# A four-part transformer kernel on one core: short last key blocks in two matmul passes, and the second batch's layer norm in smaller steps

## The chip, the cores and the metric

The kernel runs on one core of one Trainium2 chip. The metric is the device time of one execution in microseconds (us); of several runs the median is taken. The engines are called as the profile calls them: PE (matmuls; PEld is its loading of weights), DVE, ACT, POOL, and SP, whose queue issues most DMAs here.

## What is computed

The input x has 2 batches of 1024 tokens with 512 features, all in float32. Two layers follow each other; each normalises x and adds an attention and a feed-forward part to it:

```python
xn = layernorm(x)
x = x + attn0(xn) + ffn0(xn)      # one head of 128; streams mixed by a 50-step Sinkhorn chain
xn = layernorm(x)
x = x + attn1(xn) + ffn1(xn)      # 32 heads; experts by a gate
```

The change lies in the second layer's attention and in the normalisation ahead of it:

```python
q = (xn @ Wq.T)                                   # 32 heads of 128
k = (latents_k @ Wk_up.T); v = (latents_v @ Wv_up.T)   # 8 key/value heads, each for 4 query heads
scores = q @ k.T / sqrt(128);  scores = where(causal, scores, -1e9)
out = softmax(scores) @ v
x = x + out @ Wo.T + ffn1(xn)
```

The gate of ffn1 chooses two of eight experts for each token, with a capacity that is counted over both batches, so the gate of the second batch has to be known before ffn1 of the first can be computed.

## The kernel before

**Numbers in two halves.** Matmuls take float16 operands, and a float32 operand is held as a high and a low float16 part. A product needs three passes (`PASSES`, L81): high x high, high x low and low x high.

**The second layer's attention** (`layer1_attn`, L766) goes through 16 groups: 8 key/value heads for each of 2 batches. A group has 32 row steps. Row step s takes 32 queries of each of the group's 4 heads (128 rows) against the W = 32(s + 1) keys that the causal mask leaves:

- PE computes the scores (L88) into PSUM, and DVE takes the row minimum of the negated scores (L283, L287).
- ACT takes the exponential with its row sum (L291). DVE takes the reciprocal (L302).
- `rows_hi` (L301): ACT writes the high part of the normalised row (L308). `rows_lo` (L310): DVE writes the low part (L314), POOL fills what is left of the last block of 128 keys with zeros (L319), and SP transposes both parts by DMA (L320). W keys take m = ceil(W / 128) blocks of 128 for each part, 2m blocks in all.
- `attn_out` (L341) multiplies the transposed rows with the values, with V as weights, in three passes for each block of 128 keys; each matmul has 256 columns, two row steps of 128 rows (L345). `group_av` (L741) calls it for half k = 0 or 1 of query tile c: for k = 0 the two row steps have 32 and 64 keys in their last block, for k = 1 they have 96 and 128.
- ACT and DVE take the result out of PSUM in two halves (L104, L105), and PE multiplies it with Wo (L88); DVE adds it to `acc` (L737).

**What sets the order.** Beside the row steps stands a list of things to do (`fill`): each has a group and a step in which it is put, by hand. So the projections of the next group, the splitting of its weights and all the rest of the second batch's first layer are strewn over the first batch's 8 groups. `put(0, s, f)` (L1044) takes a step s counted from the first group; group 6 begins at step 192, group 7 at 224. A scheduler then orders each engine's instructions from this program. `behind(i, j, True)` (L192) makes instruction i wait for j; `last_low[0]` is the latest L314.

**The second batch's normalisation.** After the last mixing of the streams (`mix0_units`, L596, which loads each tile of x into a buffer of the tag xr, of which there are four), `late_norm` (L1038) takes the statistics of all 8 tiles at step 198 (L219, L220) and their scale and shift. At steps 200 to 207 `tile_of` (L1006) makes the transposed normalised tiles for the gate by way of `normed_T` (L227): POOL normalises (L235), ACT writes the high part into an xr buffer (L238), POOL the low part (L240), and SP transposes (L242). Three steps later each tile's gate product follows (L859). The gate's chain on DVE goes on to step 220, where `weights_of` (L916) counts both batches. At steps 231 to 238 `xT_tile` (L1002) makes the tiles again for good, half of them on POOL and half on DVE, and from 240 the latents of the second batch follow.

**Also met in the prediction:** a bias is added in the first layer's attention by matmuls with a single row (`row`, L484), followed by ordinary ones (L486).

Of the kernel before, what the change touches and what calls it, by code (L numbers as in the profile page):

```python
# [9 lines left out]
F16 = mybir.dt.float16  # L10
# [6 lines left out]
P = 128  # L17
# [19 lines left out]
FP = ((0, 2, 0, 2, 0, 2, 0, 2), (2, 2, 2, 2, 2, 2, 2, 2))  # L37
X1 = 7
CA, CB, CC, CD = 4, 1, 1, 3
SK0, SKN, MX0, MXN, LN1 = 1, 116, 122, 74, 198  # L40

G0, G1, GL, WT, LX, LA = 16, 200, 3, 220, 231, 240
AVD, WOD = 5, 10
KVN, QN, QNN, QH = 19, 18, 24, 1
FW, FF = 210, 221
BS, BP, BV = 4, 3, 1
CQ, CV = (0, 1), (0, 0)
PSCALE = 16384.0
# [3 lines left out]
def tile_model(ctx: ExitStack, tc: tile.TileContext, out: bass.AP, a: dict):  # L52
# [11 lines left out]
    def T(tag, shape, dt=F32, bufs=None):  # L64
        count[0] += 1
        kw = {} if bufs is None else {"bufs": bufs}
        return sb.tile(shape, dt, tag=tag, name=f"{tag}_{count[0]}", **kw)
# [124 lines left out]
    def behind(i, j, wait=False):  # L192

        kind = mybir.DependencyClass.Sync if wait else mybir.DependencyClass.NoSync
        tc.add_manual_dep(i.ins, j.ins.name, mybir.DependencyInfo(
            kind, mybir.DependencyReason.DATA), reason="behind")
# [14 lines left out]
        rs = C(f"rs{tag}{b}", [P, 3, NT])  # L211
        return mv, rs

    def layernorm_tiles(b, mv, rs, ts):
        ve = T("ve", [P, NT], bufs=2)
        sl = slice(ts[0], ts[-1] + 1)
        for t in ts:
            st = T("bnst", [P, 6], bufs=2)
            V.bn_stats(st, acc[b, t])  # L219
            V.bn_aggr(mv[:, t, :], st)  # L220
        V.tensor_scalar(ve[:, sl], mv[:, sl, 1], LN_EPS, None, ALU.add)
        rsqrt(rs[:, 0, sl], ve[:, sl], "rs")
        V.tensor_scalar(rs[:, 2, sl], rs[:, 0, sl], 4.0, None, ALU.mult)
        return V.scalar_tensor_tensor(rs[:, 1, sl], mv[:, sl, 0], -1.0, rs[:, 2, sl],
                                      ALU.mult, ALU.mult)

    def normed_T(b, mv, rs, t, dst, pool, tags=(("f2k", FB), ("wo", WB))):  # L227

        xn = T(tags[0][0], [P, NC, P], bufs=tags[0][1])
        xf = xn.rearrange("p c d -> p (c d)")  # L230
        hl = T(tags[1][0], [P, NC, 2, P], F16, bufs=tags[1][1])
        if pool > 1:
            A.activation(xf, acc[b, t], AF.Identity, scale=rs[:, 2, t:t + 1], bias=rs[:, 1, t:t + 1])
        elif pool:
            G.tensor_scalar(xf, acc[b, t], rs[:, 2, t:t + 1], rs[:, 1, t:t + 1], ALU.mult, ALU.add)  # L235
        else:
            V.tensor_scalar(xf, acc[b, t], rs[:, 2, t:t + 1], rs[:, 1, t:t + 1], ALU.mult, ALU.add)
        last_hi[0] = A.activation(hl[:, :, 0, :], xn, AF.Copy)  # L238
        eng = G if pool in (1, 2) else V
        lo = eng.tensor_tensor(hl[:, :, 1, :], xn, hl[:, :, 0, :], ALU.subtract)  # L240
        (last_pool if eng is G else last_lo)[0] = lo
        last_T[0] = nc.sync.dma_start_transpose(dst, hl.rearrange("p c l d -> p (c l d)"))  # L242

    def proj_T(w, xT, half):

# [20 lines left out]
    def share(got, n, k, make):  # L266

        if k % n == 0:
            got[0] = make()
        return got[0][:, k % n]  # L270
# [23 lines left out]

    def rows_parts(W, n, k):

        m = -(-W // P)
        hl = share(hl_of, n, k, lambda: T("Phl", [P, n, 2 * S // n], F16, bufs=LB))
        return hl[:, :2 * m * P].rearrange("p (l k) -> p l k", l=2)

    def rows_hi(Pm, r, W, pool, hl):  # L301
        V.reciprocal(r[:, 1:2], r[:, 0:1])  # L302
        A.activation(r[:, 1:2], r[:, 1:2], AF.Copy, scale=PSCALE)  # L303
        if pool:
            A.activation(Pm[:, :W], Pm[:, :W], AF.Copy, scale=r[:, 1:2])
            A.activation(hl[:, 0, :W], Pm[:, :W], AF.Copy)
        else:
            A.activation(hl[:, 0, :W], Pm[:, :W], AF.Copy, scale=r[:, 1:2])  # L308

    def rows_lo(Pm, r, W, pool, hl, dst):  # L310
        if pool:
            G.tensor_tensor(hl[:, 1, :W], Pm[:, :W], hl[:, 0, :W], ALU.subtract)
        else:
            lo = V.scalar_tensor_tensor(hl[:, 1, :W], Pm[:, :W], r[:, 1:2], hl[:, 0, :W],  # L314
                                        ALU.mult, ALU.subtract)
            last_low[0] = lo
        if W < hl.shape[2]:

            behind(G.memset(hl[:, :, W:], 0.0), lo)  # L319
        nc.sync.dma_start_transpose(dst, hl.rearrange("p l k -> p (l k)"))  # L320

    pending = []

# [14 lines left out]
        count[0] += 1  # L338
        return ps.tile([P, 512], F32, tag="av", name=f"av_{count[0]}", bufs=BV)

    def attn_out(p, Vh, PT, nj):  # L341

        for j in range(nj):
            for k, (l, r) in enumerate(PASSES):
                nc.tensor.matmul(p, Vh(j, l), PT(r * nj + j),  # L345
                                 start=(j == 0 and k == 0),
                                 stop=(j == nj - 1 and k == 2))


    SC0 = 1.0 / (math.sqrt(128.0) * 1024.0)  # L350
# [321 lines left out]
    def latents(b):  # L672
        cmp[b] = T("cmp", [P, NC, 2, S], F16, bufs=1)

    def lat_w(mc):
        st = T("f2k", [P, NC, P], bufs=FB)
        nc.gpsimd.dma_start(st, a["Wlat"][mc])
        w1 = T("wo", [P, 2, NC, P], F16, bufs=WB)
        split_pool(st, w1[:, 0], w1[:, 1], 32.0)
        return w1  # L680

    def fetch(src):
        st = T("f2k", [P, 512], bufs=FB)
# [54 lines left out]
        if last:  # L738
            nc.scalar.dma_start(out[(b * NT + t) * P:(b * NT + t + 1) * P, :], acc[b, t])

    def group_av(Vh, PT, c, k, p):  # L741


        attn_out(p.rearrange("p (h b q) -> p b h q", h=4, q=QR)[:, 2 * k:2 * k + 2].rearrange(
                     "p b h q -> p h b q"), lambda j, l: Vh[:, l, j, :],
                 lambda n: PT[:, n].rearrange("p b (h q) -> p h b q", q=QR), c + 1)
        if k == 0:
            return None
        ao = T("ao", [P, 2, 4, P], F16, bufs=2)
        hi, lo = [ao[:, l].rearrange("p h q -> p (h q)") for l in range(2)]  # L750
        evac(p, hi, lo, 1.0 / PSCALE)
        return ao
# [13 lines left out]
    def layer1_attn(kv0, start, extra):  # L766
# [8 lines left out]

        kvs, Qs, PTs, avs, aos, wos = [{} for _ in range(6)]

        def q_unit(g, u):
            half, hh = divmod(u, 4)
            if hh == 0:  # L780
                Qs[g, half] = T("Q", [P, 2, NS // 2, 4, QR], F16, bufs=2)
            qproj(g // NG, qw[g, hh], Qs[g, half], hh, half)
# [8 lines left out]
        def av(g, c, k):  # L791
            if k == 0:
                avs[g, c] = out_tile()
            aos[g, c] = group_av(kvs[g]["V"], PTs[g, 2 * c + k], c, k, avs[g, c])

        def wo(g, c):
            wo_block(g // NG, c, aos[g, c], [wos[g, h] for h in range(4)], g % NG == NG - 1)
# [6 lines left out]
        for g in range(N):  # L804
# [14 lines left out]
                    at(g, s, lambda g=g, hh=hh: split_wo(g + 1, hh))  # L819
            for u in range(4):  # L820
                at(g, QH + (1 if (g + 1) % NG == 0 else 3) * u, lambda g=g, u=u: q_unit(g, 4 + u))
            for c in range(NT):
                for k in range(2):
                    at(g, 4 * c + 2 * k + AVD, lambda g=g, c=c, k=k: av(g, c, k))
                at(g, 4 * c + WOD, lambda g=g, c=c: wo(g, c))
# [173 lines left out]
    def new_xT(b):  # L999
        xT1[b] = T("xT", [P, NT, 2 * NC, P], F16, bufs=1)  # L1000

    def xT_tile(b, t, pool):  # L1002
        normed_T(b, *ln1[b], t, xT1[b][:, t], pool, (("f2k", FB), ("wo", WB)) if b else
                 (("xr", XB), ("wo", WB)))

    def tile_of(b, t):  # L1006
        d = T("wo", [P, 2 * NC, P], F16, bufs=WB)
        normed_T(b, *ln1[b], t, d, True, (("f2k", FB), ("xr", XB)))
        return d

    new_xT(0)
# [23 lines left out]
    gw1 = gating_w()  # L1035
    chain = sinkhorn(1, logit[1])

    def late_norm():  # L1038
        ln1[1] = layernorm(1, "b")
        layernorm_tiles(1, *ln1[1], range(NT))  # L1040

    extra = {}

# [11 lines left out]
    for t in range(NT):  # L1055
        for k, f in enumerate(mix0_units(1, t, f0[1][5], True)):
            put(0, MX0 + MXN * (4 * t + max(k - 1, 0)) // 32, f)
    for t in range(NT):
        put(1, 2 * t, lambda t=t: branch0_add(1, t, y4s[t], f0[1][4]))
    hs, gates, dts, lw = {}, {}, {}, {}  # L1060
# [5 lines left out]
    def gate_step(b):  # L1066
        next(gates[b], None)

    for b, s in ((0, G0), (1, G1)):
        put(0, s, lambda b=b: gate_start(b))  # L1070
        for t in range(NT):
            if b == 0:
                put(0, s + t, lambda t=t: gating_h(hs[0], t, gw1, xT1[0][:, t]))
            else:
                put(0, s + t, lambda t=t: dts.update({t: tile_of(1, t)}))
                put(0, s + t + GL, lambda t=t: gating_h(hs[1], t, gw1, dts[t]))
        for k in range(10):
            put(0, s + NT + GL + k, lambda b=b: gate_step(b))
    put(0, LN1, late_norm)
    put(0, WT, weights_of)  # L1080
    put(0, LX, lambda: new_xT(1))
    for t in range(NT):
        put(0, LX + t, lambda t=t: xT_tile(1, t, t % 2 == 1))

    def lat_unit(mc, th):
        if mc + th == 0:
# [1 line left out]
        lat_evac(1, mc, th, lat_block(1, lw[mc], th))  # L1088

    for mc in range(4):  # L1090
        put(0, LA + 2 * mc - 4, lambda mc=mc: lw.update({mc: lat_w(mc)}))
        for th in range(2):
            put(0, LA + 2 * mc + th, lambda mc=mc, th=th: lat_unit(mc, th))
    for k in range(6):
        for s in (FW, 8 * 58 + 2):
            put(0, s + 2 * k - 2, lambda k=k: ffn_fetch(k))
            put(0, s + 2 * k, lambda k=k: ffn_split(k))
    for t in range(NT):
        put(0, FF + t, lambda t=t: ffn_block(0, t))
        put(60, 4 * t + 3, lambda t=t: ffn_block(1, t))  # L1100
# [48 lines left out]
```

## Time and profile before

| | |
|---|---|
| median of 3 runs | 1860.09 us (1855.35 to 1863.01) |
| the profiled execution, its own time | 1855.46 us |
| its span in the profile | 1853.7 us |
| mean granted clock | 0.976 |
| DVE, ACT, POOL busy | 78%, 64%, 49% of the span |
| L345, matmuls with the values | 3648, 447.7 us busy, 274 ns mean |
| L314, low parts of rows | 515, 434.4 us busy, 853 ns mean |
| L319, fills with zeros | 384, 72.6 us busy |
| L320, transposes of rows | 528, 3.2 us median to landing |

A busy time is the sum of the instructions' spans on an engine. Matmuls overlap each other in it, so that 274 ns is how long one of L345 was in the engine, not how far it is from the next. The first layer ends near 250 us, the first batch's eight groups fill the time to about 950 us, and the second batch's the rest.

### The profile page before, as it was taken

What the parts mean: (1) busy time and instruction counts of PE and PEld (TensorE: products, weight loads), DVE (VectorE), ACT (ScalarE), POOL (GpSimd) and SP (SyncE); (2) the same over time, 40 slices, a digit from 0 to 9 for tenths busy, and PEclk for the clock granted to TensorE, in tenths of its full rate; (3) what the DMA queues carried; (4) which work ended last, traced back from release to release, by engine and by line L of the source; (5) the groups of instructions that cost most, each with busy time, mean ns of one, the idle gap of its engine ahead of it and who ended that gap; (6) DMA issues with size and microseconds to landing.
All of it is one profiled execution on the core that took longest, in us unless ns stands there. A gap on an engine that the chain in (4) does not pass through costs nothing. (4 is left out here: it accounts for less than half of the span.)

```text
span 1853.7 us, 35094 instructions
## 1 busy us (share of the span) xinstructions
PE 1715.7 (93%) x11458; PEld 1046.0 (56%) x11458; DVE 1447.6 (78%) x4050; ACT 1194.1 (64%) x2917; POOL 910.6 (49%) x1540
## 2 busy tenths in 40 slices
PE   4756399999999999998999999999999999999998
PEld 3434146566666556655555556666666666656565
DVE  8888978988888877777976867777777777777675
ACT  3848665656676778776544756666666767676554
POOL 5567639768775455647634333424242433335200
PEclk9878699999999999999999999999999999999999
DMA  7435225666574657468546555656565656566455
GB/s 211 82 56 124 67 51 131 143 115 144 113 147 102 143 115 158 111 131 158 137 92 141 130 120 126 146 111 150 107 151 115 142 117 140 117 141 139 101 123 120
DMA packets 707306, 230.26 MB, mean 124 GB/s; under 512 B 689953, under 2 KB 690081, under 8 KB 707122
## 3 DMA queue, kind: packets, MB, share of 16 engines
q1 hardware_dynamic: 691666, 180.75, 47.2%
q0 software_dynamic: 13152, 43.07, 8.5%
q10 hardware_dynamic: 2304, 4.20, 0.7%
q8 instruction: 90, 1.47, 0.4%
q14 instruction: 94, 0.77, 0.1%
HBM read 52.81 MB, written 4.19 MB: 31 GB/s over the span
## 5 line engine op out<-in xcount | busy, mean ns | idle before, releaser
L291 ACT ACTIVATE P<-P,nm 128x1024 f32<-128x1024 f32 (+31 forms) x528 | 391.3, 742 | 250.0 <-DVE nm L283 234.8
L314 DVE SCALAR_TENSOR_TENSOR Phl<-P,r,Phl 128x1024 f16<-128x1024 f32 (+31 forms) x515 | 434.4, 853 | 85.9 <-ACT Phl L308 79.5
L88 PE MATMUL s<-K,Q 128*128 128x512 f16 (+22 forms) x2400 | 440.7, 317 | 19.5 <-DVE P L287 11.6
L345 PE MATMUL av<-PT,V 128*128 128x256 f16 x3648 | 447.7, 274 | 7.5 <-DMA PT<-Phl 6.8
L345 PEld LDWEIGHTS <-V 128*128 128x128 f16 x3648 | 357.0, 98 | 94.7 <-DMA PT<-Phl 8.3
L308 ACT ACTIVATE Phl<-P,r 128x1024 f16<-128x1024 f32 (+31 forms) x515 | 370.0, 731 | 22.3 <-DMA PT<-Phl 3.3
L88 PE MATMUL pp<-xT,wq 128*128 128x512 f16 x1536 | 372.9, 381 | 6.3 <-DVE acc L737 3.2
L88 PE MATMUL pp<-wo,ao 128*128 128x512 f16 x1536 | 369.9, 379 | 2.9 <-ACT ao L104 2.7
L94 POOL TENSOR_SCALAR f2k<-f2k 128x512 f32<-128x512 f32 x164 | 109.5, 668 | 499.9 <-DVE Phl L314 444.5
L88 PEld LDWEIGHTS <-Q 128*128 128x128 f16 x2400 | 223.2, 98 | 178.2 <-issue 28.4
L88 PEld LDWEIGHTS <-wq 128*128 128x128 f16 x1536 | 149.6, 98 | 173.8 <-issue 8.5
L88 PEld LDWEIGHTS <-ao 128*128 128x128 f16 x1536 | 149.4, 98 | 156.5 <-ACT ao L104 4.8
L287 DVE TENSOR_SCALAR_CACHE_REDUCE P<-s 128x512 f32<-128x512 f32 (+15 forms) x272 | 152.6, 562 | 21.7 <-PE s L88 19.7
L283 DVE CUSTOM_DVE_ANT_0 P<-s,mask,nm 128x272 f32<-128x272 f32 (+15 forms) x256 | 157.3, 615 | 8.7 <-PE s L88 1.0
L303 ACT ACTIVATE r<-r 128x1 f32<-128x1 f32 x528 | 96.2, 193 | 66.2 <-DVE r L302 65.4
L319 POOL MEMSET Phl<- 128x192 f16 (+2 forms) x384 | 72.6, 209 | 133.5 <-DMA PT<-Phl 95.7
L302 DVE RECIPROCAL r<-r 128x1 f32<-128x1 f32 x528 | 79.2, 155 | 75.3 <-ACT P L291 72.1
L104 ACT ACTIVATE ao<-av 128x512 f16<-128x512 f32 x128 | 75.1, 587 | 92.2 <-PE av L345 92.0
L283 DVE CUSTOM_DVE_ANT_0 P<-s,mask 128x32 f32<-128x32 f32 (+15 forms) x256 | 104.3, 432 | 27.6 <-PE s L88 27.1
L104 ACT ACTIVATE Q<-pp 128x512 f16<-128x512 f32 x128 | 74.5, 582 | 76.7 <-PE pp L88 72.2
L737 DVE SCALAR_TENSOR_TENSOR acc<-pp,acc 128x512 f32<-128x512 f32 x128 | 87.4, 682 | 41.0 <-PE pp L88 40.6
L105 DVE SCALAR_TENSOR_TENSOR Q<-pp,Q 128x512 f16<-128x512 f32 x128 | 87.6, 684 | 34.9 <-ACT Q L104 34.6
(254 smaller groups left out, 2119.1 us busy)
## 6 DMA issues: line engine op xcount, KB each, us to landing
f2k<-in_Wq POOLq DMA_DIRECT2D x64, 256.0 KB, 3.2
f2k<-in_WoT POOLq DMA_DIRECT2D x64, 256.0 KB, 3.3
PT<-Phl SPq DMA_TRANSPOSE x528, 3.2
acc<-in_x SPq DMA_DIRECT2D x16, 256.0 KB, 4.6
f2k<-in_Wup POOLq DMA_DIRECT2D x16, 256.0 KB, 3.5
out<-acc ACTq DMA_DIRECT2D x16, 256.0 KB, 3.5
xr<-in_x SPq DMA_DIRECT2D x12, 256.0 KB, 4.1
f2k<-in_Wlat POOLq DMA_DIRECT2D x8, 256.0 KB, 5.5
```

The lines of the kernel that those rows point to most:

```text
L88: nc.tensor.matmul(dst, lhs(l), rhs(r), start=(i == 0 and j == 0), stop=(i == n - 1 and j == 2))
L94: first = G.tensor_scalar(stage, stage, scale, 1.0, ALU.mult, ALU.mult)
L104: A.activation(hl_hi, src, AF.Copy, scale=scale)
L105: return V.scalar_tensor_tensor(hl_lo, src, scale, hl_hi, ALU.mult, ALU.subtract)
L283: last_row[0] = V.tensor_tensor_reduce(Pm[:, o:o + w], pt[:, :w], mask[:, 512 - w:], -scale, first, ALU.add, ALU.min, nm[:, k:k + 1])
L287: last_row[0] = V.tensor_scalar(Pm[:, o:o + w], pt[:, :w], -scale, first, ALU.mult, ALU.min, accum_out=nm[:, k:k + 1])
L291: A.activation(Pm[:, :W], Pm[:, :W], AF.Exp, bias=last, scale=-1.0, accum_out=r[:, 0:1])
L303: A.activation(r[:, 1:2], r[:, 1:2], AF.Copy, scale=PSCALE)
L308: A.activation(hl[:, 0, :W], Pm[:, :W], AF.Copy, scale=r[:, 1:2])
L314: lo = V.scalar_tensor_tensor(hl[:, 1, :W], Pm[:, :W], r[:, 1:2], hl[:, 0, :W], ALU.mult, ALU.subtract)
L345: nc.tensor.matmul(p, Vh(j, l), PT(r * nj + j), start=(j == 0 and k == 0), stop=(j == nj - 1 and k == 2))
L737: V.scalar_tensor_tensor(acc[b, t], p, 1.0 / 256.0, acc[b, t], ALU.mult, ALU.add)
```

## The change

**Two passes for a short last block.** Where the last block has at most 64 keys (the first two row steps of every four), `rows_parts` now lays the last block out as 64 columns of high part and 64 columns of low part, so that a row has 2c + 1 blocks instead of 2c + 2 (c full blocks stand before the last). The low part is then written by two DVE instructions where c > 0: one for the full blocks, one for the last. Only rows with 32 keys in the last block have something to fill with zeros. On PE the last block takes two matmuls: one with all 128 rows, whose weights `Vm` hold the high part of the block's first 64 values twice, and one with 64 rows, for the low part of the values. `twice` copies the values for it, by two DMAs on SP for each group, into a buffer of the tag xr.

```diff
     def rows_parts(W, n, k):
+        c, w = divmod(W, P)
+        hl = share(hl_of, n, k, lambda: T("Phl", [P, n, 2 * S // n], F16, bufs=LB))
+        if 0 < w <= 64:
+            hl = hl[:, :(2 * c + 1) * P]
+            o = c * P
+            lo = [(o, W, hl[:, o + 64:o + 64 + w])]
+            if c:
+                lo.insert(0, (0, o, hl[:, o + P:]))
+            pad = hl[:, o:o + P].rearrange("p (l k) -> p l k", l=2)[:, :, w:] if w < 64 else None
+            return hl, hl[:, :W], lo, pad
...
     def rows_lo(Pm, r, W, pool, hl, dst):
...
+        for a0, a1, lo in los:
...
+                last_low[0] = V.scalar_tensor_tensor(lo, Pm[:, a0:a1], r[:, 1:2], hi[:, a0:a1],
+                                                     ALU.mult, ALU.subtract)
+        if pad is not None:
+            behind(G.memset(pad, 0.0), last_low[0])
+        nc.sync.dma_start_transpose(dst[:, :whole.shape[1] // P], whole)
...
+    def attn_out(p, Vh, PT, nj, mixed=None):
+        full = nj - (mixed is not None)
+        todo = [(Vh(j, l), PT(r * nj + j)) for j in range(full) for l, r in PASSES]
+        if mixed is not None:
+            todo += [(mixed, PT(full)), (Vh(full, 1)[:64], PT(full)[:64])]
+        for k, (v, pt) in enumerate(todo):
+            nc.tensor.matmul(p, v, pt, start=(k == 0), stop=(k == len(todo) - 1))
...
+        def twice(g):
+            Vm = kvs[g]["Vm"] = T("xr", [P, NT, P], F16, bufs=XB)
+            for k in range(2):
+                nc.sync.dma_start(Vm[64 * k:64 * k + 64], kvs[g]["V"][0:64, 0])
...
+            at(g, 2, lambda g=g: twice(g))
```

**The second batch's norm.** Each tile's statistics come three steps after its last mixing (`late_stats`); what is left of `late_norm` goes to step 197. Making a tile is cut in two: the normalising and the high part in one step, the low part and the transpose in the next (`later`). POOL's two instructions of a tile wait for the latest L314 (L381 is the new line of L345, L347 that of L314). Tiles 1, 4 and 7 are normalised on ACT instead of POOL, and the steps are no longer one after the other:

```diff
-G0, G1, GL, WT, LX, LA = 16, 200, 3, 220, 231, 240
+G0, GL, WT, LX, LA = 16, 2, 221, 231, 240
+G1 = (198, 199, 200, 201, 203, 204, 205, 207)
+GP = (1, 2, 1, 1, 2, 1, 1, 2)
+G2 = 210
...
-FW, FF = 210, 221
+FW, FF = ((210, 212, 213, 215, 216, 218), tuple(8 * 58 + 2 + 2 * k for k in range(6))), 222
...
-            G.tensor_scalar(xf, acc[b, t], rs[:, 2, t:t + 1], rs[:, 1, t:t + 1], ALU.mult, ALU.add)
+            xg = G.tensor_scalar(xf, acc[b, t], rs[:, 2, t:t + 1], rs[:, 1, t:t + 1], ALU.mult, ALU.add)
+            if later is not None:
+                behind(xg, last_low[0], True)
...
+        def low():
+            lo = eng.tensor_tensor(hl[:, :, 1, :], xn, hl[:, :, 0, :], ALU.subtract)
+            if eng is G and later is not None:
+                behind(lo, last_low[0], True)
+            (last_pool if eng is G else last_lo)[0] = lo
+            last_T[0] = nc.sync.dma_start_transpose(dst, hl.rearrange("p c l d -> p (c l d)"))
...
+        put(0, MX0 + MXN * (4 * t + 3) // 32 + 3, lambda t=t: late_stats(t))
...
-                put(0, s + t, lambda t=t: dts.update({t: tile_of(1, t)}))
-                put(0, s + t + GL, lambda t=t: gating_h(hs[1], t, gw1, dts[t]))
+                put(0, G1[t], lambda t=t: dts.update({t: tile_of(1, t, lambda f: lows.update({t: f}))}))
+                put(0, G1[t] + 1, lambda t=t: lows.pop(t)())
+                put(0, G1[t] + GL + 1, lambda t=t: gating_h(hs[1], t, gw1, dts[t]))
```

The tiles that are made for good (`xT_tile`, step 231 on) are cut in the same way. The weights of the second batch's latents are fetched two steps before they are split, and their splitting waits for the latest L314; the weights of ffn1 are split at slightly other steps for the first batch, and the counting and ffn1 come one step later.

## Prediction

> **What bounds the kernel now.** I read the page's busy shares and slices first, then the busy time by stretch, then TensorE's waits, then the timeline where TensorE changes from one kind of matmul to the next.
>
> ```profile
> PE 1715.7 (93%) x11458; PEld 1046.0 (56%) x11458; DVE 1447.6 (78%) x4050; ACT 1194.1 (64%) x2917; POOL 910.6 (49%) x1540
> ...
> PE   4756399999999999998999999999999999999998
> ```
>
> From slice 7 on PE is full. A busy PE need not be PE at its peak, so I checked by stretches (span; PE, PEld, DVE, ACT, POOL busy; granted clock):
>
> ```profile
> 250.00:820.00 570.00, 558.90 (x3776) 343.67 (x3775) 470.79 (x1318) 402.75 (x1034) 364.79 (x693) 1.00 0.57 124
> 820.00:950.00 130.00, 115.46 (x838) 72.16 (x837) 107.64 (x287) 72.62 (x176) 86.29 (x120) 0.96 0.69 145
> 1090.00:1840.00 750.00, 748.98 (x4995) 464.14 (x4993) 556.45 (x1523) 487.33 (x1168) 252.07 (x466) 1.00 0.60 129
> ```
>
> In the second batch (1090 to 1840) PE idles 1.0 us in 750; in the first (250 to 820) 11.1 us in 570, and DVE is 83% busy there. Between them, where the second batch is normalised, 14.5 of 130 us are idle. The timeline of PE (start, length, group) in a full stretch gives the price of a matmul:
>
> ```profile
> 1458.08 2.78 PE L345 MATMUL av<-PT,V 128*128 128x256 f16 x24
> 1460.70 2.32 PE L88 MATMUL pp<-wo,ao 128*128 128x512 f16 x10
> 1462.86 0.38 PE L88 MATMUL pp<-xT,wq 128*128 128x512 f16 x1
> ```
>
> Start to start, 24 of L345 take 2.62 us: 109 ns each; ten of 512 columns take 2.16 us: 216 ns. That is streaming with nothing between, and whatever shortens PE's stream in these stretches shortens the span.
>
> **Part 1: two passes instead of three.** For each group, query tile and first half (16 x 8 = 128 times) the three 256-column matmuls of the last key block become two. Removed: 128 x 109 ns = **14.0 us**, all on PE.
>
> The second of the two is new in kind: it uses 64 rows, and every matmul around it 128. In the built order each of the 128 stands between 128-row matmuls, so there are 256 changes of row count. No 64-row matmul is in this trace; the nearest rows are the 1-row bias matmuls of L484. PE, then PEld:
>
> ```profile
> 189.42 0.82 PE L345 MATMUL av<-PT,V 128*128 128x256 f16 x6
> 190.17 1.46 PE L484 MATMUL pp<-wo,row 1*128 1x512 f16 x6
> ...
> 192.83 1.03 PE L486 MATMUL pp<-wo,wo 128*128 128x512 f16 x4
> 194.21 0.59 PE L484 MATMUL pp<-wo,row 1*128 1x512 f16 x2 [0.35 <-DVE acc L488]
> 194.73 0.82 PE L486 MATMUL pp<-wo,wo 128*128 128x512 f16 x3
> ```
>
> ```profile
> 193.78 0.09 PEld L484 LDWEIGHTS <-row 1*128 1x128 f16 x1 [0.42 <-issue]
> 194.21 0.09 PEld L484 LDWEIGHTS <-row 1*128 1x128 f16 x1 [0.33 <-issue]
> 194.72 0.33 PEld L486 LDWEIGHTS <-wo 128*128 128x128 f16 x3 [0.42 <-issue]
> ```
>
> Within one row count the next weights load while the matmul before streams: the second L484 load starts at 194.21, with the first matmul. At a change they don't. Into one row: four L486 from 192.83 stream until 192.83 + 4 x 0.216 = 193.69, and the load starts at 193.78, 0.09 late; in the other place 189.42 + 6 x 0.109 = 190.07, and L484 starts at 190.17, 0.10 late. Out of it: 194.21 + 2 x 0.216 = 194.64, and L486 starts at 194.73, 0.09 late; the idle time before its load is put down to issue alone. So a pair of changes costs about 0.19 us, more than the 109 ns that the removed matmul saves. If 64 rows behave like one, 128 x 0.19 = **24.3 us** are added; if changing from 128 to 64 is free, nothing. Below nothing is excluded: a 64-row matmul still streams 256 columns. I take 24.3, the only row of a change there is, and keep 0 for the range.
>
> The Trainium skill has a rule that speaks against this part: "TensorEngine Tiling (Array Packing)", Key Properties, says that a change of tiling mode (128, 64 or 32 rows), not of the tile alone, drains TensorE. It names no price and counts 64 rows as a mode of its own. By the rule the cost is paid; without it 24.3 us would be nothing.
>
> On DVE the low part of a row step with 32 or 64 keys in its last block becomes two instructions where full blocks stand before it: 14 a group, 224 in all. The rows for L314 by shape:
>
> ```profile
> L314 DVE SCALAR_TENSOR_TENSOR Phl<-P,r,Phl 128x1024 f16<-128x1024 f32 x19 | 25.4, 1335 | 2.9 <-ACT Phl L308 2.9
> L314 DVE SCALAR_TENSOR_TENSOR Phl<-P,r,Phl 128x512 f16<-128x512 f32 x16 | 13.3, 834 | 4.2 <-ACT Phl L308 4.1
> L314 DVE SCALAR_TENSOR_TENSOR Phl<-P,r,Phl 128x32 f16<-128x32 f32 x16 | 5.2, 328 | 0.9 <-ACT Phl L308 0.8 <-issue 0.2
> ```
>
> (1335 - 834) / 512 = 0.98 ns an element, so a 32-element instruction is 328 - 31 = 297 ns of overhead, with what it waited for POOL inside; the shortest L314 in the trace took 231, so at least 200. 224 x 0.2 to 0.3 = 45 to 67 us of DVE work, 3 to 4 us in each group of 91.8 us (PE's timeline has the twelve L345 of 1407.60 again from 1499.39 on). In the second batch DVE is 74% busy and PE covers it: nothing. In the first batch DVE goes from 83% to about 87%, and PE's waits for DVE between 250 and 820 (most of the 11.1 us idle) can grow; without cover the worst is that they double. I take +2, between 0 and +11.
>
> At nothing I cost these: 128 fewer memsets of 209 ns and 128 shortened from 263 to 156 (POOL 34% busy after 1090); 16 fewer of 288 transposed blocks a group (PE's waits for them are 6.8 us in the whole run, so that is the most they give); and 32 copies of the first 64 rows of each block of values, two a group, on SP between the transposes. There a copy waits for the evacuation of V, and the next transposes stand behind it. SP issues 32 transposes of 1.3 us in 92 us, so two issues of about 0.6 us fit; if each group lost as much as one such issue on PE, it would be 16 x 0.6 = 10 us.
>
> **Part 2: the second batch's norm.** The statistics (8 x (682 + 169) ns = 6.8 us of DVE) move from one step near 830 us to eight earlier steps; nothing is added. The normalised tiles go in two steps, with the low part and the transpose one step later; POOL's part waits for the last low part on DVE; three of eight tiles are normalised on ACT. The stretch it touches, and PE's waits in it:
>
> ```profile
> 850.00:900.00 50.00, 44.14 (x366) 27.60 (x364) 37.44 (x94) 27.09 (x63) 34.93 (x48) 0.93 0.81 159
> ```
>
> ```profile
> PE pp L88 <- DVE acc L737: 3.2, 1, 3.2
> PE pp L88 <- DVE Phl L314: 2.7, 1, 2.7
> ```
>
> 5.9 us idle, and a granted clock of 0.93 after the gaps costs 44.1 x 0.07 = 3.1 us: **8.9 us** lost in the steps that normalise the tiles. The first wait is behind three L314 that took 4.3 us while POOL ran L235 and L240. The second goes back by way of DVE (3.0 us for ACT L291) to ACT L238, which waited 2.1 us for the transpose that frees an xr buffer. The later start of POOL, five of its eight first steps instead of eight, and transposes that in the built order stand at five places among the group's row transposes rather than three, speak for a gain of up to 8.9. Against it: the copies of V now hold one of the four xr buffers all the time and the gating's h another, so the tiles have two instead of three, and the second wait is of that kind. One more such pair of waits would cost 4.4. I take half of the loss, -4.4, between -8.9 and +4.4. What is late next if both waits go is the gating chain: PE's waits for it between 900 and 950 add up to 2 us.
>
> **Sum.** -14.0 + 24.3 + 2 - 4.4 = **+7.9 us** on the profiled execution's 1855.46 us (span 1853.7 and 1.8 around it): 1863.4. That execution is one of the faster; the median of the three runs is 1860.09, 4.6 above it, and the changed kernel should vary alike, so I forecast 1868. This is +0.43%; about 0.5%, or 9.3 us, is what a measurement of this kernel can tell from no change.
>
> **Rivals.**
> - *64 rows change for free* (0.18). For it: no 64-row matmul is in the trace, and one row is the extreme case. Against: the load that isn't pulled ahead is seen both ways and in each place. Then -14.0 + 0 + 2 - 4.4 = -16.4: 1844, faster. It decides by price: below 14.0 / 256 = 55 ns a change, part 1 gains.
> - *DVE becomes the bound of the first batch* (0.25). Place: the row steps of groups 0 to 6, where PE already waits for the row minimum and for Q. If the 20 us or so of new DVE work there doubles the 11.1 us of PE idle, and the tiles find no free xr buffer (0 instead of -4.4), it is -14.0 + 24.3 + 11 + 0 = +21: 1881, clearly slower. It decides from where DVE's share there comes to about 90%. Against: the stretches between waits are long and PE gets slower too.
> - *The middle recovers all* (0.12): with changes paid, -14.0 + 24.3 + 2 - 8.9 = +3.4: 1863.5, no change.
> - *Fewer matmuls that move nothing* can't be: the built order has 11330 instead of 11458, and PE is the bound from 250 us on.
>
> **How the numbers follow.** The forecast, 1868, has chance 0.45 and a range of its own from 1864 (DVE at 0, the middle at -6.5) to 1875 (DVE at +5, the middle at 0). Slower by over 0.5% is above 1869.4: 0.20 of the forecast case and the DVE rival's 0.25, together 0.45. Within 0.5%: the other 0.25 of the forecast case and 0.10 of the full recovery, 0.35. Faster: the free change, 0.18, and 0.02 of the full recovery, where a change costs less than the row says: 0.20. The range over all cases, 1843 to 1883, takes in the free change (1844) and the DVE rival (1881), with 1 or 2 us for the spread of the median.
>
> **What would show it.** In the profile after: L381 (the old L345) with 3520 matmuls, 128 of them with 64 rows; before and after each of these, in the second batch, start-to-start gaps near 0.20 us instead of 0.109 (forecast), or 0.109 (free change). A group of the second batch (8 fewer matmuls, 8 pairs of changes) would take 91.8 - 0.87 + 1.52 = 92.4 us, or 90.9. PE's waits for DVE between 250 and 820 near 13 us, against 22 in the DVE rival. In the steps of the tiles, L238 waiting for a transpose says that two xr buffers are too few; no PE wait above 1 us and a clock of 1.00 say that the two steps work. I would be wrong above all if 64 rows were no mode of their own, or if a change costs more where the neighbours are 256 columns wide.

## The result, and the profile after

The changed kernel takes **1870.31 us** in the median (1865.73 to 1875.18, 8 runs), the kernel before, run beside it, 1861.88 us (1855.35 to 1864.77, 8 runs). The ratio is **1.0053**, 95% interval 1.0032 to 1.0073: 6 to 14 us slower. The forecast was 1868. Below, the us of a run are its ratio to the kernel before, run beside it, times 1860; for this one +9.9.

The profiled execution of the changed kernel takes 1871.81 us (span 1870.0). That is 16.4 above the profiled one of before, which lies 6.4 below its own median: differences read from two traces can be off by some us, and the medians decide.

The page's busy shares and slices, after:

```profile
PE 1730.8 (93%) x11330; PEld 1022.3 (55%) x11330; DVE 1503.2 (80%) x4274; ACT 1195.1 (64%) x2920; POOL 874.1 (47%) x1409
...
PE   4766399899999999998999999999999999999998
```

TensorE has 128 matmuls fewer and is busy 15.1 us longer; DVE has 224 instructions more. By stretches (span; PE, PEld, DVE, ACT, POOL busy; granted clock):

```profile
250.00:820.00 570.00, 560.39 (x3704) 332.57 (x3703) 488.20 (x1394) 397.81 (x1022) 352.53 (x645) 0.99 0.57 121
820.00:950.00 130.00, 116.92 (x828) 69.77 (x826) 112.38 (x307) 81.90 (x192) 75.85 (x105) 0.97 0.62 142
1090.00:1840.00 750.00, 749.50 (x4891) 448.33 (x4890) 577.13 (x1624) 481.42 (x1168) 236.49 (x402) 1.00 0.58 124
```

PE is as full as before in the first and last row, but gets fewer matmuls done in the same time: 3704 for 3776, 4891 for 4995. Of the 72 and 104 that are missing, the change itself takes away 8 a group, about 48 and 65. The timeline shows where it goes. PE, then PEld, in a group of the second batch; `av<-PT,xr` is the new first pass, the 64-row form the second:

```profile
1473.77 2.46 PE L381 MATMUL av<-PT,V 128*128 128x256 f16 x21
1476.06 0.27 PE L381 MATMUL av<-PT,xr 128*128 128x256 f16 x1
1476.27 0.28 PE L381 MATMUL av<-PT,V 64*128 64x256 f16 x1
1476.48 2.33 PE L91 MATMUL pp<-wo,ao 128*128 128x512 f16 x10
```

```profile
1475.96 0.10 PEld L381 LDWEIGHTS <-xr 128*128 128x128 f16 x1
1476.26 0.09 PEld L381 LDWEIGHTS <-V 64*128 64x128 f16 x1 [0.21 <-issue]
```

Twenty-one matmuls from 1473.77 to 1476.06 are 109 ns each. The step into the 64-row matmul is 0.21 us and the step out of it 0.21 again. The weights of the 128-row pass load before their matmul (1475.96 for 1476.06), those of the 64-row pass only when it can start. Over all 128 places the trace gives 205 ns in and 212 out (medians), and the matmul after the next starts 10 ns late (226 ns for 216, where both have 512 columns): 96 + 103 + 10 = **209 ns a pair** of changes, 26.8 us in the whole kernel.

Much of what follows rests on one table, worked out from the traces: the length of each stretch in us. The first layer is counted from PE's first instruction; a group lasts from its first score matmul of 32 columns to that of the next (the last one to its last matmul).

| profiled execution of | first layer | groups 0-5 | groups 6+7 | groups 8-15 |
|---|---|---|---|---|
| before | 238.8 | 562.0 | 262.2 | 763.4 |
| after | 241.1 | 565.4 | 266.0 | 770.1 |
| e1: 64 rows in the third pass | 241.3 | 568.2 | 259.9 | 776.5 |
| e2: after with 128 rows | 237.5 | 561.7 | 265.0 | 757.2 |
| e3: two passes alone | 241.2 | 565.6 | 271.6 | 770.2 |
| e4: norm steps alone | 238.0 | 562.4 | 263.8 | 763.4 |
| e5: split low part | 239.3 | 572.1 | 271.1 | 765.7 |
| e6: copies | 238.1 | 567.0 | 266.1 | 764.0 |
| e7: one pass dropped | 240.5 | 563.8 | 264.4 | 756.1 |
| e8: second batch alone, 128 rows | 238.9 | 563.2 | 259.2 | 755.9 |
| e9: other order | 239.5 | 561.3 | 262.9 | 763.0 |
| e10: e5 in e9's order | 237.4 | 572.6 | 269.8 | 765.6 |
| e11: e3 with 128 rows | 240.0 | 561.6 | 270.7 | 756.3 |
| e12: e8 and norm steps | 239.1 | 562.0 | 265.6 | 757.3 |

The first layer is the same work in all rows and spreads over 4 us, so a difference of 2 or 3 us in the first batch's columns, from one trace each, is not clear. Groups 8 to 15 repeat within 1.5 us wherever the same is computed there in the same way.

### The profile page after: what moved, and what is told of

It reads as the page before. It is cut to its first block, busy times and chain, and to the rows that moved or that the text cites. A ratio compares the mean times of both kernels' runs of the same rounds, so it can differ in the third digit from the quotient of the medians.

```text
span 1870.0 us, 35011 instructions
## 1 busy us (share of the span) xinstructions
PE 1730.8 (93%) x11330; PEld 1022.3 (55%) x11330; DVE 1503.2 (80%) x4274; ACT 1195.1 (64%) x2920; POOL 874.1 (47%) x1409
## 5 line engine op out<-in xcount | busy, mean ns | idle before, releaser
L347 DVE SCALAR_TENSOR_TENSOR Phl<-P,r,Phl 128x64 f16<-128x64 f32 (+9 forms) x739 | 490.4, 697 | 69.6 <-ACT Phl L339 65.2
L381 PE MATMUL av<-PT,V 128*128 128x256 f16 (+1 forms) x3392 | 440.0, 275 | 11.7 <-DMA PT<-Phl 10.2
L381 PEld LDWEIGHTS <-V 128*128 128x128 f16 (+1 forms) x3392 | 331.1, 98 | 121.3 <-issue 32.8
L91 PEld LDWEIGHTS <-wq 128*128 128x128 f16 x1536 | 148.9, 98 | 172.2 <-issue 6.6
L91 PEld LDWEIGHTS <-ao 128*128 128x128 f16 x1536 | 143.5, 98 | 165.8 <-ACT ao L107 5.5
L305 DVE TENSOR_SCALAR_CACHE_REDUCE P<-s 128x512 f32<-128x512 f32 (+15 forms) x272 | 152.8, 563 | 13.7 <-PE s L91 11.1
L99 POOL TENSOR_TENSOR wo<-f2k,wo 128x512 f16<-128x512 f32 x84 | 102.1, 1216 | 4.3
```

The lines of the kernel that those rows point to most:

```text
L91: nc.tensor.matmul(dst, lhs(l), rhs(r), start=(i == 0 and j == 0), stop=(i == n - 1 and j == 2))
L99: G.tensor_tensor(hl_lo, stage, hl_hi, ALU.subtract)
L305: last_row[0] = V.tensor_scalar(Pm[:, o:o + w], pt[:, :w], -scale, first, ALU.mult, ALU.min, accum_out=nm[:, k:k + 1])
L347: last_low[0] = V.scalar_tensor_tensor(lo, Pm[:, a0:a1], r[:, 1:2], hi[:, a0:a1], ALU.mult, ALU.subtract)
L381: nc.tensor.matmul(p, v, pt, start=(k == 0), stop=(k == len(todo) - 1))
```

## The experiments

The theory after the result: the forecast is near because a pair of changes costs what it said. The rival: it is near because of errors that cancel, since DVE's work and groups 6 and 7 had only been bounded. Each ratio below is to the kernel before, with its 95% interval.

### What a change of row count costs: e1 and e2

e1 is the kernel before, with its third pass over the last block cut to 64 rows for the first half (the other 64 rows are zeros). e2 is the changed kernel with all rows in the second pass.

```diff
 e1 (before)
-                nc.tensor.matmul(p, Vh(j, l), PT(r * nj + j),
+                n = 64 if short and j == nj - 1 and k == 2 else P
+                nc.tensor.matmul(p, Vh(j, l)[:n], PT(r * nj + j)[:n],
 e2 (after)
-            todo += [(mixed, PT(full)), (Vh(full, 1)[:64], PT(full)[:64])]
+            todo += [(mixed, PT(full)), (Vh(full, 1), PT(full))]
```

> The kernel before, with one thing changed: the third pass over the last key block of each k = 0 half (low part of the values, high part of the row) goes over the block's first 64 rows instead of 128. No matmul is removed and the result is the same. Theory (a change of row count costs PE its stream): the gaps in the changed kernel's trace are 205 ns into a 64-row matmul and 212 ns out of it instead of 109, and 10 ns at the next start, so 209 ns a pair and 128 pairs: +26.8 us, ratio 1.0144. Rival (the changed kernel's loss comes from its layout, DVE's extra instructions or the copies on SP, and the gaps are covered): +0.

> The changed kernel, with its 64-row matmul over all 128 rows of the same two tiles. It adds a product of two low parts (of other keys) of the size of the one that three passes leave out anyway; nothing else differs. Theory: the 256 changes go, 26.8 us less than the changed kernel: about -18 us against the kernel before, ratio 0.990. Rival (other costs of the new layout make the loss): it stays at +8, ratio 1.005.

Measured: e1 1876.1 us, ratio 1.0087 [1.0069, 1.0104], **+16.2**; e2 1854.27, 0.9965 [0.9953, 0.9978], **-6.5**, that is 16.4 below the changed kernel. In e2's trace, at a like place, the step is 0.11 us:

```profile
1472.69 0.27 PE L381 MATMUL av<-PT,xr 128*128 128x256 f16 x1
1472.80 0.27 PE L381 MATMUL av<-PT,V 128*128 128x256 f16 x1
```

So the changes cost 16 us, not nothing and not the 26.8 that the gaps add up to: in both runs theory and rival are missed, and the measured value lies between them. The table says where the rest is: groups 8 to 15 hold 64 pairs, 13.4 us, and pay 13.1 (e1) and 12.9 (after less e2). Groups 0 to 5 hold 48 pairs, 10.0 us, and pay 6.2 and 3.7; groups 6 and 7 hold 16 and pay nothing clear (-2.3 and +1.0). In the first batch, lengthening PE's stream costs about a third of its length.

### The two parts apart: e3, e4 and e11

e3 is part 1 of the diff alone, with the norm of before; e4 is part 2 alone; e11 is e3 with e2's line (`Vh(full, 1), PT(full)` in the second pass).

> The two passes alone; the second batch's norm as in the kernel before. Theory: 26.8 - 14.0 = +12.8 us on PE, ratio 1.0069, and the norm's part was worth the 4.4 us that are missing to the changed kernel's +8.4. Rival (the norm's part is worth nothing, and part of PE's loss hides in its idle time): +8.4, ratio 1.0045. If the copies crowd the old tiles' xr buffers, above +13.

> The second batch's norm in smaller steps alone, with three passes. Theory: -4.4 us, ratio 0.9976, with group 6 some 4 us shorter. With no copies of V the tiles have three xr buffers, so if the buffers matter the gain is larger, up to -8.9 (0.995). Rival (no effect outside one execution): 0.

> Two passes alone (e3_part1, with the norm of the kernel before), the second pass with all 128 rows, which adds a product of low with low part. It is the fourth corner beside e3_part1 (64 rows, old norm: +17.1), the changed kernel (64 rows, new norm: +8.4) and e2_rows128 (128 rows, new norm: -6.5). Theory: the two parts add up, the norm in steps is worth 7 to 9 us wherever the first batch has two passes, so without changes of row count it is 16 us below e3_part1: about +1 us against the kernel before. Rival: the norm in steps only gets back what the changes of row count cost around it, and is worth nothing without them: about -6.5 us. Groups 8 to 15 take 90.9 us each by both.

Measured, with e2 and the changed kernel as the other corners:

| | 64 rows | 128 rows |
|---|---|---|
| norm of before | e3: 1.0089 [1.0073, 1.0106], +16.6 | e11: 1.0008 [0.9993, 1.0023], +1.5 |
| norm in steps | after: 1.0053 [1.0032, 1.0073], +9.9 | e2: 0.9965 [0.9953, 0.9978], -6.5 |

e4: 0.9996 [0.9984, 1.0008], -0.7.

The parts add up: the changes cost 15 and 16 us in both rows, the norm in steps gains 6.7 and 8.0 in both columns. That is what e11's theory expected, and its rival (-6.5) fell. e3 came out above both of its numbers, which its expectation puts down to the copies crowding the tiles out of the xr buffers. The traces of e3 and e11 show that wait grown, and the prediction had bounded it. In groups 6 and 7 of e11, ACT's high parts of the tiles wait for the transpose that frees a buffer (us in total, times, longest):

```profile
ACT xr L238 <- DMA wo<-xr: 6.0, 4, 2.2
```

It is 6.2 us in e3 and 4.1 after. Before, it was:

```profile
ACT xr L238 <- DMA wo<-xr: 2.7, 2, 2.1
```

e6 below has the copies too, but 2.6 us; so the copies alone don't make it.

Alone, in e4, the norm in steps gains nothing, as the rival had it. In the trace of e4 group 6 takes 114.8 us instead of 122.2, and group 7 148.9 instead of 140.1. PE in group 7 of e4 (L363 is the old L345), and SP's queue there (L338 transposes rows, L255 the tiles made for good):

```profile
1008.50 0.57 PE L91 MATMUL s<-K,Q 128*128 128x320 f16 x3
1015.52 2.74 PE L363 MATMUL av<-PT,V 128*128 128x256 f16 x12 [6.45 <-DMA PT<-Phl]
```

```profile
991.04 2.58 SPq L338 DMA_TRANSPOSE PT<-Phl  x2
993.72 13.73 SPq L255 DMA_TRANSPOSE xT<-wo  x6
1007.50 5.29 SPq L338 DMA_TRANSPOSE PT<-Phl  x2
```

SP issues one after another: the two row transposes that PE waits for were issued behind six tile transposes, from 1007.50 on. They landed at 1014.04 and 1015.48, each about 6.5 us after its issue where the median is 3.2, just after the last of the six (1013.29), and PE stood still for 6.45 us. The tile transposes in the queue are not enough for such a wait: before, all eight stood there in a row,

```profile
995.72 17.41 SPq L242 DMA_TRANSPOSE xT<-wo  x8
```

and PE waited for no row transpose from 985 to 1060. So it must also matter what PE has left to do meanwhile, which no run tests. What the first tiles gain in group 6 (7.4 us) is lost again in group 7 (8.8), which has this wait. How much time falls to which of the two also depends on the order: e9 below, which changes nothing in the norm, moves 3 to 4 us from group 6 to group 7. With two passes in the first batch the balance is another: the old norm then costs groups 6 and 7 about 271 us (e3, e11) instead of 262, and the steps bring them back to 265 or 266 (e2, after). With the steps these two groups take 264 to 266 whatever else is changed.

### What the first batch pays: e5 to e8

e5 writes the low part in two instructions where the last block has 32 or 64 keys, as the changed kernel does, and e6 makes the copies and uses them as weights; both keep three passes and the old layout. e7 drops the third pass of the last block for the first half. e8 has the two passes at 128 rows, with their split and copies, in the second batch's groups only (`short[0]` is set there).

```diff
 e5 (before)
-            lo = V.scalar_tensor_tensor(hl[:, 1, :W], Pm[:, :W], r[:, 1:2], hl[:, 0, :W],
-                                        ALU.mult, ALU.subtract)
+            o = W // P * P if 0 < W % P <= 64 else 0
+            for a0, a1 in ((0, o), (o, W)) if o else ((0, W),):
+                lo = V.scalar_tensor_tensor(hl[:, 1, a0:a1], Pm[:, a0:a1], r[:, 1:2],
+                                            hl[:, 0, a0:a1], ALU.mult, ALU.subtract)
 e6 (before)
+            at(g, 2, lambda g=g: twice(g))
...
-                     "p b h q -> p h b q"), lambda j, l: Vh[:, l, j, :],
+                     "p b h q -> p h b q"), lambda j, l: Vm[:, j] if k == 0 and j == c and l == 0 else Vh[:, l, j, :],
 e7 (before)
-            for k, (l, r) in enumerate(PASSES):
+            todo = PASSES[:2] if short and j == nj - 1 else PASSES
+            for k, (l, r) in enumerate(todo):
 e8 (after, norm of before, 128 rows)
-        if 0 < w <= 64:
+        if short[0] and 0 < w <= 64:
```

> The kernel before, with the low part of a row written by two DVE instructions where the last block has 32 or 64 keys and full blocks stand before it; layout and everything else as before, the result the same. It isolates the changed kernel's 224 more DVE instructions. Theory (DVE bounds the first batch's groups, so its extra work shows there): +5 us, all between 250 and 950, nothing after 1090. Rival, which the prediction held (PE covers it): +0 to +2.

> The kernel before, with the two copies of V's first rows for each group, in a buffer of the tag xr, taken as weights of the first pass over the last block of a k = 0 half; the rows against which the copied half stands are zeros there, so the result is the same. It isolates the copies and the buffer that they hold. Theory (the tiles of the second batch's norm have two buffers instead of three): +5 to +9 us in groups 6 and 7, ACT's wait of L238 for a transpose up from 2.7 us to 6 or more, and nothing after 1090. Rival (buffers enough): 0.

> The kernel before without the third pass over the last key block of a k = 0 half: it leaves out the product of the low part of those values with the high part of the rows. 128 matmuls of 109 ns go and nothing is added. If PE bounds both batches, as the prediction held: -14.0 us. Theory now (the first batch is bound by DVE for part of its groups): -7.0 us after 1090 and -2 to -4 before it, so about -10.

> Two passes with 128 rows in both, in the second batch's groups alone; the first batch and the second batch's norm as before. Like the run with 128 rows it adds a product of two low parts. Theory: the second batch gets the 64 matmuls' 7.0 us and the first pays neither DVE's nor the copies' price: -6 to -7 us, about what two passes of 128 rows gave in both batches together. Rival (the first batch gains too where PE is the bound there): clearly less gain than that run's 6.5.

Measured: e5 1.0099 [1.0081, 1.0117], **+18.4**; e6 1.0038 [1.0022, 1.0055], +7.1; e7 0.998 [0.9965, 0.9995], -3.7; e8 1850.86 us, 0.9951 [0.9933, 0.997], **-9.1**.

Against what was expected, e5 lies far above its theory (+5) and its rival (0 to +2). e6 has the total of its theory, but 5.0 of the us in groups 0 to 5, and the wait of L238 did not grow. e7 stays above both of its numbers (-14 and -10). e8 gains somewhat more than its theory's 6 to 7, which lie in its interval (-12.5 to -5.6).

*The pass.* By the table e7 gains 7.3 us in groups 8 to 15, the 64 x 109 ns = 7.0 of its matmuls there, while groups 0 to 7 get no shorter (4.0 longer). PE's busy time and its waits in the first batch, of e7:

```profile
250.00:820.00 570.00, 552.38 (x3702) 336.59 (x3700) 472.16 (x1311) 398.31 (x1024) 357.37 (x691) 0.99 0.58 124
```

```profile
PE s L88 <- DVE nm L283: 6.1, 5, 2.4
PE s L88 <- DVE P L287: 2.8, 3, 2.0
PE pp L88 <- DVE acc L738: 2.3, 2, 1.6
PE pp L88 <- ACT ao L104: 1.9, 2, 1.1
```

Before, these were (there was no wait for `acc`):

```profile
PE s L88 <- DVE nm L283: 5.0, 6, 1.3
PE s L88 <- DVE P L287: 2.0, 2, 1.0
PE pp L88 <- ACT ao L104: 0.2, 1, 0.2
```

(The waits are given in total, times and longest.) PE is busy 6.5 us less than before in this stretch (558.90), and idles 6.5 more: its waits there add up to 17.3 us instead of 11.1, those for row minima to 8.9 instead of 7.0, and the ones for `acc` and ACT's `ao` have grown as much. So PE at 98% was not what set the time there by itself. The prediction had ruled this out as a rival ("Fewer matmuls that move nothing can't be").

*The split.* e5 loses 10.1 us in groups 0 to 5, 8.9 in 6 and 7, and 2.3 in the second batch. These 2.3 are in the last group; groups 8 to 14 take 91.8 us each as before, so there PE covers the split. In the first batch PE waits more for DVE; e5, 250 to 820:

```profile
PE s L88 <- DVE nm L283: 5.6, 5, 2.0
PE s L88 <- DVE P L287: 4.9, 4, 2.4
PE pp L88 <- DVE acc L739: 2.6, 2, 1.4
```

These are 13.1 us, against 7.0 for the minima before and none for `acc`.

*The copies.* e6 loses 5.0 us in groups 0 to 5, about what a single wait of PE takes:

```profile
365.06 1.39 PE L88 MATMUL s<-K,Q 128*128 128x192 f16 x12
372.25 4.02 PE L345 MATMUL av<-PT,V 128*128 128x256 f16 x18 [5.80 <-DMA PT<-Phl]
```

The row transpose that ends it was issued at 364.68 and landed at 372.21, 7.5 us later where the median is 3.2; a fetch of Wq that POOL issued beside it (364.98) took 6.1 us, also against 3.2. No copy stands in SP's queue there (the nearest are issued at 301.62 and 408.22, 1.18 us for two). So this wait is not the copies' own time; why the transfers took so long there is not shown, and neither is what makes up the 3.9 us in groups 6 and 7.

*The place.* e8 shows that in the second batch the two passes are worth their matmuls, with the split and the copies in it: -9.1 us, and groups 8 to 15 at 755.9, 7.5 below before and as in e7. Adding the same to the first batch (e11) makes it 10.6 us slower, all of it in groups 6 and 7 (259.2 to 270.7).

### Order or work: e9, e10 and e12

Each edit lets the scheduler find another order, so e5's price could be that of an order. e9 only lets the Sinkhorn chain end two steps earlier; e10 is e5 with that. e12 is e8 with the norm in steps.

```diff
 e9, e10 (before, e5)
-SK0, SKN, MX0, MXN, LN1 = 1, 116, 122, 74, 198
+SK0, SKN, MX0, MXN, LN1 = 1, 114, 122, 74, 198
```

> The kernel before, with its Sinkhorn chain spread over steps 1 to 114 instead of 1 to 116 (SKN). No work is added or taken away; the scheduler puts some 9400 of TensorE's instructions in another place. Open is why splitting the low part on VectorE (e5_dvesplit) cost 18 us in the first batch, where the added work is at most 2 x 20 us on an engine that is 83% busy. Theory 'work': the order alone moves the time little, within 3 us of the kernel before (1857 to 1863 where that is 1860), and e5's 18 us are VectorE's. Rival 'order': any edit that makes the scheduler find another order in the first batch moves the time by several us: 5 to 18 us on either side, nearly all of it in groups 0 to 7.

> The split of the low part on VectorE (the edit of e5_dvesplit) together with the Sinkhorn chain over 114 steps (the edit of e9_order). Theory 'work': the split costs the same 18 us on top of the other order, so 15 to 21 us above e9_order. Rival 'order': the 18 us belonged to the one order that the scheduler made; here the split costs something else, 0 to 8 us above e9_order. In both, groups 8 to 15 stay at 91.8 us each.

> The best version so far (e8_batch1: two passes with 128 rows in the second batch's groups only; this adds the product of low with low part there) and the norm in steps. The norm in steps was worth 0.7 us alone (e4_part2), because what group 6 gained group 7 gave back. Theory: the first batch here is that of e4_part2, so again it is worth nothing: -9 to -10 us against the kernel before. Rival: it is worth 7 us as in the changed kernel: -16 us.

Measured: e9 1.0006 [0.9994, 1.0019], +1.1; e10 1.0097 [1.0075, 1.012], +18.0, which is 16.9 above e9; e12 0.9968 [0.995, 0.9985], -6.0. The other order moves no stretch of the table by more than 0.7 us (inside the third, group 6 takes 118.9 us instead of 122.2 and group 7 144.1 instead of 140.1), and the split costs nearly the same in it, in the same stretches (11.3, 6.9 and 2.6 us): the rival 'order' fell, for this order. e12 agrees with 'worth nothing' for the norm in steps where the first batch has three passes, and the rival (-16) fell; groups 6 and 7 even take 6.4 us more than in e8, and the whole 3.1 more by the ratios, with intervals that overlap. It shows e4's wait again, 6.8 us for row transposes in group 7.

*What stays open.* The prices of the first batch don't add up. Singly in groups 0 to 7, e5 loses 19.0 us, e6 8.9 and e7 4.0; together, in e11, they lose 8.1. In groups 6 and 7 the split alone (8.9) is as much as e11's 8.5, so that the copies (3.9 in e6) would add nothing to it. In groups 0 to 5 e11 loses nothing, though the split alone loses 10.1. What pays for it there, the shorter fills on POOL, the shorter transposes or the dropped pass behind a longer DVE, wasn't tried.

## Why the prediction came out near, step by step

The runs make a chain from before to after, one step of the sum at a time, each the quotient of two ratios:

| step | predicted | measured | from |
|---|---|---|---|
| two passes, second batch | -7.0 | -9.1 | e8 |
| two passes, first batch: -7.0, DVE +2, copies 0 | -5.0 | +10.6 | e11 against e8 |
| changes of row count | +24.3 | +15.1 | e3 against e11 |
| norm in steps | -4.4 | -6.7 | after against e3 |
| sum | +7.9 | +9.9 | |

The sum was right to 2 us, with two steps wrong by 16 and 9 us in opposite directions; so the rival of cancelling errors holds for the total, and the theory for the price. That the total came out near was luck.

**The price of a change** was right: 0.19 us from a row of one-row matmuls, 0.209 at 64 rows. The gaps of 0.20 us that the prediction named are there, and a group of the second batch takes 92.7 us (mean of those without the last) where 92.4 was forecast. The rule of the Trainium skill in "TensorEngine Tiling (Array Packing)", Key Properties, that a change of tiling mode drains TensorE, agrees with this trace: the gaps are there at 64 rows (205 and 212 ns) and gone at 128 (109). The rival of a free change (1844) fell.

**"Whatever shortens PE's stream in these stretches shortens the span"** is the step that failed. It holds for the second batch, where PE idled 1.0 us in 750: the gain of the pass and the cost of the changes came out there to 1 or 2 us. In the first batch PE idled 11.1 us in 570, and DVE was 83% busy; there neither the 7.0 us removed came back (e7) nor the 13.4 us added were paid in full (about 4 to 5). What PE saves there goes mostly to waits for DVE (e7), and the 98% did not show that they were next. So the changes cost 15.1 us instead of 24.3 by their place, not by their price.

**DVE at +2 and the copies at nothing** were mis-sized. The instruction's price was right: L347 in 250 to 820 is 80 more instructions and 16.5 us more than L314 was, 0.21 us each, within 0.2 to 0.3. The cover was not there: the split alone costs 18.4 us (e5), more than the worst that the prediction allowed for (11). PE's waits for DVE in that stretch did not show it, though: in the changed kernel they are lower than before, 6.9 us in all instead of 10.2. After, 250 to 820:

```profile
PE s L91 <- DVE nm L301: 3.7, 4, 2.1
PE pp L91 <- ACT ao L107: 1.9, 2, 1.2
PE s L91 <- DVE P L305: 1.5, 2, 1.2
PE av L381 <- DVE ao L108: 1.0, 2, 0.7
```

These had been expected near 13 us, or 22 in the DVE rival. The copies alone cost 7.1 us (e6); what they cost beside the split is not known. That they leave the tiles two xr buffers instead of three did not show by itself: L238 waits 2.6 us in e6 and 2.7 before. The DVE rival had the right sign for the first batch and named the row steps of groups 0 to 6; the loss sits in groups 6 and 7, where the statistics, the tiles and the gate come on top. There e11, where nothing is paid for changes, has PE busy 111.63 us instead of 115.46 before, and a granted clock of 0.93 instead of 0.96. PE waits there 3.3 us for the tiles' transposes, for which it did not wait before, and 2.7 instead of 1.3 for the gate's chain:

```profile
820.00:950.00 130.00, 111.63 (x787) 68.97 (x786) 110.48 (x300) 73.65 (x176) 80.34 (x110) 0.93 0.70 142
```

**The norm in steps** gained 6.7 us, within its bounds of -8.9 and +4.4. That is its gain beside the two passes in the first batch; beside three it is nothing (e4), or a loss that is not clear of the noise (e12). As what is late next the prediction named the gate's chain (1.7 us of PE's waits after). More goes to the tiles' transposes, and in e4 and e12 to SP's queue in group 7 (6.5 and 6.8 us). The waits in the steps of the tiles, after:

```profile
PE pp L91 <- DMA wo<-xr: 3.8, 2, 3.1
PE av L381 <- DMA PT<-Phl: 2.9, 2, 2.3
PE s L91 <- DVE nm L301: 2.7, 2, 1.6
```

The first line is the gate's product waiting for a tile's transpose, 3.1 us at the longest: above the 1 us that would have said that the steps work as meant.

Of all versions e8 is the fastest: 9.1 us below the kernel before (5.6 to 12.5) and 19 below the changed one. It leaves the first batch as it was.

## What to carry to other kernels

Price a step apart for each stretch, by whether an engine there idles at all: at 1 us idle in 750 a stream is priced by its matmuls; at 11 in 570, with another engine at 83%, neither taking work away nor adding it to the first engine moves the time by its length. A matmul over fewer rows saves nothing here when it stands alone among full ones: pad it with rows that may be multiplied (e2), or put many of one kind together, which was not tried. And when two steps of a sum have opposite signs, test each alone before trusting a total that came out right.

## What the runs showed of the hardware

A single 64-row matmul of 256 columns among 128-row ones has gaps of 205 ns before and 212 ns behind it instead of 109, at 127 of 128 places with next to no spread (the 10th and 90th percentile are 205 and 205, 211 and 213; one has 646 behind it). Its weights start to load 0.20 us after the start of the matmul before, where 128-row weights load 0.10 us ahead of their own matmul. At 0.209 us a pair, a change to 64 rows costs nearly what the one to a single row cost before (0.19).
